# Four edits in a two-layer graph network: a type mask read from a table, a leaky ReLU through TensorE, node stores on ScalarE's queue, and sums begun by a copy

## The chip, the cores and the metric

The kernel runs on one core of a Trainium2 chip. The metric is the time of one execution on the device, in microseconds (us). The kernel before has a median of 4184.74 us over three runs (4179.8 to 4191.42). In this text PE is the matrix engine (TensorE), DVE the vector engine, ACT the scalar engine, POOL the GpSimd engine and SP the sync engine, which here does little but start transfers. DRAM is the memory outside the core; SBUF and PSUM are the two memories on it.

## The reference

There are 6250 nodes with 128 features and 106,250 edges, sorted by destination. The second layer takes the same edge list. Cut to what is computed (`relu`, `leaky` and `segment` functions written short):

```python
h = relu(layernorm(x))
for r in range(4):                              # edge types; 8 heads of 16 features
    xr = (h @ W_rel[r]).reshape(N, 8, 16)
    es, ed = (xr * a_src[r]).sum(-1), (xr * a_dst[r]).sum(-1)
    logit = leaky(es[src] + ed[dst], 0.2)
    logit = where(edge_type == r, logit, -1e30)
    p = exp(logit - segment_max(logit, dst)[dst]) * (edge_type == r)
    alpha = p / segment_sum(p, dst)[dst]
    out_r = segment_sum(alpha * xr[src], dst) + bias[r]
    h_r = gelu(out_r) @ W_cross
ent = stack([h @ W_self, h_0, h_1, h_2, h_3])   # 5 x N x 128
# a softmax over these five per node and head (types without an edge at a node left out)
x = x + sum_k(alpha_k * ent[k]) + bias_lang

h = relu(layernorm(x))
src2, dst2, ef2 = concat(src, dst), concat(dst, src), concat(ef, ef)
msg = leaky(concat(h[src2], h[dst2], ef2) @ We1, 0.01) @ We2
red = segment_sum(msg, dst2)
x = x + leaky(concat(h, red) @ Wn1, 0.01) @ Wn2
```

## The kernel before

**Tiling.** Nodes are cut into 50 blocks of 126 (two halves of 63, so 100 halves). The edges of a half are at most 1152, nine tiles of 128. Four halves make a superblock: 25 superblocks of nine steps. In each step one tile of each of the four halves is handled, so a step has four gathers and layer 1 has 900.

**Preparation** (0 to 167 us in the profile). The edge lists are loaded as 128x832 arrays on SP's queue, `x` on ACT's. DVE makes small edge tables in DRAM (`e2`, `turnd`, `dtyp`: what node and type an edge has, where a run of equal destinations ends). The first edge of each half is found (`st0`). Then 50 blocks of node rows go through layer norm and PE, and the projected rows of all four types are stored as a table `xt`, the node's own rows as `own`. Last, the indices of the gathers (`xi`) and the one-hot keys (`key`) are turned into place.

**Layer 1** (167 to 1578 us). `gather0` fetches the rows of `xt` for the edges, by an indirect DMA that POOL issues (L81), 17 tiles ahead of their use (18 buffers, `xg`). While superblock s has its messages made, superblock s + 1 has its softmax prepared:

- `loads`, two superblocks ahead, on SP's queue: for each of the four halves a slice of `turnd` (tile `t`), of `dst` and of `dtyp` spread over 64 partitions (`db`, `dt`), and of the edge types spread over four partitions (`et`).
- `masks`: DVE compares `et` with the partition's type number `tycf` (L508), which gives `ne`, 1 where an edge has another type; and `db` with the node numbers (L512), which gives the one-hot `oT`.
- `logits`, in three chunks of 384 edges: PE adds, in one PSUM bank `lg`, −1e30 times `ne` (L523), the destination's part (L525) and, after an ACT copy `es` for each tile, the source's part. There is one buffer of `lg`. The leaky ReLU is the larger of lg and 0.2 lg: ACT multiplies (L532), DVE takes the maximum (L533), both into `l`.
- `soft`: four scans of DVE along the edges with exponentials and a logarithm on ACT; `turn`: PE brings the weights to edges by partitions (`pt`).
- `messages`, each step of superblock s: DVE multiplies the gathered rows by the weights (L583), makes four one-hots (L590), and PE adds their products into `acc` (L591). `types` (L598) finds on ACT which types a node has.
- `nodes`, spread over the steps of the next superblock as a generator: gelu, the product with `W_cross`, the softmax over the five, the sum with ps in PSUM (copied to `y`), layer norm, and the second layer's products. It stores `y` to `x1r` (L684, two transfers), the two halves of the node table of layer 2 `abtab` (L703, four) and `h2t` (L704, one), all from SP's queue, behind a later point of the generator than that at which the data is made.

**Layer 2** (1578 to 4196 us). For each of 50 blocks and nine steps, POOL gathers two tiles of `abtab` rows (`ag`, ten buffers), PE makes the rest of the sum `z` (L1037) from the edge features `fe` and a one-hot of the destination (`db`, L999), DVE adds (L1039), ACT multiplies by 0.01 (L1040), DVE takes the maximum (L1041), and POOL stores the result row by row, sorted by the source node, to `m2d` (L1045). The destination's own sum is made by PE (`sums`, L1055), added to `racc` once a block (L1065). Behind each of five parts of the blocks, `windows` reads `m2d` back by source node and adds those sums to `racc` as well (L956). `racc` holds 50 blocks of 128x256 and is cleared by POOL before the layer (L924). After the last part, `node_update` makes the output, four blocks at a time.

**Order.** The order within the loops is written out by hand, as the generators and the step numbers above; a scheduler of the framework then orders the instructions of each engine by their dependences, and inserts the waits. Each engine and each queue runs in order.

Of the kernel before, what the change touches and what calls it, by code (L numbers as in the profile page):

```python
# [9 lines left out]
F32 = mybir.dt.float32  # L10
BF16 = mybir.dt.bfloat16
I32 = mybir.dt.int32
U8 = mybir.dt.uint8
AF = mybir.ActivationFunctionType
ALU = mybir.AluOpType
# [6 lines left out]
P = 128  # L22
# [4 lines left out]
R = 4  # L27
# [7 lines left out]
J = 832  # L35
# [50 lines left out]
def kernel(ctx: ExitStack, tc: tile.TileContext, x, src, dst, ef, et, w_rel, a_src, a_dst,  # L86
# [14 lines left out]
    def dram(name, shape, dt=F32):  # L101
        return nc.dram_tensor(name, shape, dt, kind="Internal").ap()
# [7 lines left out]
    turnd = dram("turnd", (2, JE + 8), BF16)  # L110
    dtyp = dram("dtyp", (1, JE))
    plcd = dram("plcd", (1, JE))
    m2d = dram("m2d", (E + TRASH, MW))
# [78 lines left out]
    with ExitStack() as prep:  # L192
# [84 lines left out]
        for k in range(2):  # L277
            nc.sync.dma_start(turnd[k, 1:JE + 1].rearrange("(p j) -> p j", j=J), dn[:, k, :])
            for o, w in ((0, 1), (JE + 1, 7)):
                nc.sync.dma_start(turnd[k:k + 1, o:o + w], dn[0:1, k, 0:w])  # L280
        dty = cpool.tile([P, J], F32, name="dty")
        stt(dty, dstf, float(R), ints["et"], op0=ALU.mult, op1=ALU.add)
# [150 lines left out]
    with ExitStack() as s1_:  # L433
# [6 lines left out]
        nc.gpsimd.iota(iota, [[1, R * 64]], base=0, channel_multiplier=0, allow_small_or_imprecise_dtypes=True)  # L440
        tyc = cp.tile([Q * R, 1], I32, name="tyc")
        nc.gpsimd.iota(tyc, [[0, 1]], base=0, channel_multiplier=1)
        ts_(tyc, tyc, R - 1, None, op0=ALU.bitwise_and)
        tycf = cp.tile([Q * R, 1], F32, name="tycf")
        nc.vector.tensor_copy(tycf, tyc)
        pen = cp.tile([Q * R, P], BF16, name="pen")
# [40 lines left out]
        def loads(s):  # L487
            ln = {}
            regs = first_of(st0, Q * s, Q, E - CAP)
            ln["t"] = wp.tile([2 * Q, CAP + 2], BF16, name="t")  # L490
            ln["et"] = wp.tile([Q * R, CAP], I32, name="et")
            ln["db"] = [wp.tile([P, CAP], I32, name="db") for _ in range(2)]
            ln["dt"] = [wp.tile([P, CAP], F32, name="dt") for _ in range(2)]
            for q in range(Q):
                r = regs[q]
                v, h0 = q // 2, (q % 2) * 64
                nc.sync.dma_start(ln["t"][2 * q:2 * q + 2, :], turnd[:, ds(r, CAP + 2)])
                nc.sync.dma_start(ln["db"][v][h0:h0 + 64, :], dst[ds(r, CAP)].partition_broadcast(64))
                nc.sync.dma_start(ln["et"][q * R:(q + 1) * R, :], et[ds(r, CAP)].partition_broadcast(R))
                nc.sync.dma_start(ln["dt"][v][h0:h0 + 64, :], dtyp[0, ds(r, CAP)].partition_broadcast(64))  # L500
            lanes[s] = ln

        def masks(s):

            ln = lanes[s]
            ln["a"] = wp.tile([P, CAP], F32, name="a", bufs=1)
            ln["ne"] = wp.tile([Q * R, CAP], BF16, name="ne", bufs=1)
            ts_(ln["ne"], ln["et"], tycf, None, op0=ALU.not_equal)  # L508
            ln["oT"] = []
# [7 lines left out]
        def logits(s, c):  # L517
# [9 lines left out]
            for i in range(3):  # L527
# [3 lines left out]
                                 start=False, stop=(i == 2), skip_group_check=True)  # L531
            nc.scalar.mul(ln["l"][:, e0:e1], lg, 0.2)  # L532
            tt(ln["l"][:, e0:e1], lg, ln["l"][:, e0:e1], op=ALU.max)  # L533

# [85 lines left out]
        def nodes(s, g, gt, last):  # L620

            e5 = wp.tile([P, R + 1, 2, C + H], F32, name="e5", bufs=1)
            rows = own[2 * s * P:(2 * s + 2) * P, :].rearrange("(v p) c -> p v c", v=2)
# [37 lines left out]
            y = wp.tile([P, 2, C], F32, name="y", bufs=1)  # L661
            nc.scalar.copy(y, ps)
            yield
            bn = wp.tile([P, 2, 6], F32, name="bn")
# [15 lines left out]
            for v in range(2):  # L680
                ts_(h2[:, v, :], ps[:, v, :], mv[:, v, 0:1], r[:, 0, v:v + 1], op0=ALU.subtract, op1=ALU.mult)
            x1q = x1r[2 * s * DB:(2 * s + 2) * DB, :].rearrange("(v q r) c -> q r v c", v=2, q=2)
            for q in range(2):
                nc.sync.dma_start(x1q[q], y[q * 64:q * 64 + GB])  # L684
            yield
# [3 lines left out]
            hT = wp.tile([P, 2 * P], F32, name="hT2")  # L689
            nc.scalar.activation(hT, tp, AF.Relu)  # L690
            yield

            ab = abtab[2 * s * DB:(2 * s + 2) * DB, :].rearrange("(v q r) f -> v q r f", v=2, q=2)
            for v in range(2):
                at = wp.tile([P, 2 * HID], F32, name="at")
                ps = bank(last)
                for a in range(2):
                    nc.tensor.matmul(ps[:, a * HID:(a + 1) * HID], hT[:, v * P:(v + 1) * P], wab[:, a, :],
                                     start=True, stop=True)
                nc.scalar.copy(at, ps)  # L700
                yield
                for q in range(2):
                    nc.sync.dma_start(ab[v, q], at[q * 64:q * 64 + GB])  # L703
            nc.sync.dma_start(h2t[:, 2 * s * P:(2 * s + 2) * P], hT)  # L704

# [207 lines left out]
    with ExitStack() as s4:  # L913
# [9 lines left out]
        col = col.rearrange("p q r -> p (q r)")  # L923
        nc.gpsimd.memset(racc, 0.0)  # L924

        def windows(j):
# [17 lines left out]
            for b in range(NU):  # L944
# [7 lines left out]
                for i in range(n):  # L952
                    oh = mp.tile([P, P], F32, name="ohw", bufs=4)
                    ts_(oh, col, at[:, i:i + 1], None, op0=ALU.is_equal)  # L954
                    nc.tensor.matmul(sums, oh, mt[:, i, 0:HID], start=(i == 0), stop=(i == n - 1))  # L955
                tt(racc[:, b, :], racc[:, b, :], sums, op=ALU.add)  # L956
                yield

        with ExitStack() as s5:
# [59 lines left out]
            for u in range(NU):  # L1019
# [43 lines left out]
                for _ in nxt_:  # L1063
                    pass
                tt(racc[:, u, :], racc[:, u, :], sums, op=ALU.add)  # L1065
            for _ in wins:
# [586 lines left out]
```

## Time and profile before

The profile is of one execution of 4198.35 us; its span (first to last instruction) is 4196.5 us, with 1.85 us around it. The median of the three timed runs is 4184.74 us.

| what | value |
|---|---|
| time, median of 3 (lowest, highest) | 4184.74 us (4179.8, 4191.42) |
| profiled execution, its span | 4198.35 us, 4196.5 us |
| mean granted TensorE clock | 0.848 |
| preparation, to the first gather | 0 to 167.2 us |
| layer 1, first to last gather | 167.2 to 1453 us |
| rest of layer 1 | 1453 to 1578.5 us |
| layer 2, first gather to POOL's last store | 1589.8 to 3993.8 us |
| last part and node update | 3993.8 to 4196.5 us |
| busy: PE, DVE, ACT, POOL | 3081.6, 2896.6, 1518.3, 2939.8 us |

How to read the profile's lines: the first line gives each engine's busy time, its share of the span and its number of instructions. A group line gives source line, engine, operation, result and operands by the program's names, the count, then busy time and the mean of one in ns, then the idle time of the engine just before them and what ended most of it. A line of the timeline gives start, length (us), engine, source line, operation, and in brackets the idle time before it with its releaser; "issue" is time in which the engine waited for nothing that the profile shows. L81 is the helper that issues every gather.

### The profile page before, as it was taken

The page shows a single profiled execution, that of the slowest core. Times are in us where ns is not written, and L with a number is a line of the kernel's source. Part 1 is how long each engine was busy: PE and PEld are TensorE (multiplying, and loading weights), DVE is VectorE, ACT ScalarE, POOL GpSimd, SP SyncE. Part 2 cuts the span into 40 slices and gives each one's busy share as a digit, 9 for nine tenths or more (in the row PEclk, how much of TensorE's full clock was granted, in tenths as well). Part 3 has the DMA queues.
Part 4 walks back from the last instruction along what each step waited for, and adds up shares of the span by engine and source line. Part 5 has one row for each costly group of instructions (what it writes and reads, how often), then busy time and mean ns, then how long its engine had stood idle before and what let it go on. Part 6 is the DMA issues. An engine that isn't in the chain of part 4 may idle for free. (4 is left out here: it accounts for less than half of the span.)

```text
span 4196.5 us, 43288 instructions
## 1 busy us (share of the span) xinstructions
PE 3081.6 (73%) x11108; PEld 1776.0 (42%) x11108; DVE 2896.6 (69%) x5392; ACT 1518.3 (36%) x2861; POOL 2939.8 (70%) x2889
## 2 busy tenths in 40 slices
PE   3457777777777765666677877778768777688888
PEld 2345555555555552222234433344324333244455
DVE  6777899999887764455566666566656666577755
ACT  2256655665555532222222322222222222222211
POOL 4777777777777607777777777777777777777700
PEclk9767888778778777888889999889988998899999
DMA  6645544444445317666678887787868878588754
GB/s 169 166 100 119 114 116 116 114 116 115 112 114 121 91 47 208 175 172 181 171 216 240 252 247 208 220 257 239 241 193 259 246 238 248 170 262 272 242 163 137
DMA packets 414125, 754.31 MB, mean 180 GB/s; under 512 B 182798, under 2 KB 248948, under 8 KB 413868
## 3 DMA queue, kind: packets, MB, share of 16 engines
q0 software_dynamic: 148800, 430.91, 35.4%
q1 hardware_dynamic: 247350, 307.89, 27.9%
q10 hardware_dynamic: 17718, 12.66, 1.2%
q8 instruction: 91, 1.49, 0.1%
q14 instruction: 166, 1.36, 0.1%
HBM read 587.35 MB, written 163.84 MB: 179 GB/s over the span
## 5 line engine op out<-in xcount | busy, mean ns | idle before, releaser
L81 POOL DMA_INDIRECT xg<-xt,xi x900 | 1005.1, 1117 | 280.8 <-issue 232.3
L1045 POOL DMA_INDIRECT m2d<-s,placei x900 | 915.8, 1018 | 288.7 <-issue 210.7
L81 POOL DMA_INDIRECT ag<-abtab,srci x900 | 911.4, 1013 | 288.2 <-issue 205.2
L1037 PE MATMUL z<-rhs,lt 128*128 128x512 f32 x1800 | 1041.1, 706 | 0.6 <-ACT lt L1008 0.6
L1041 DVE TENSOR_TENSOR s<-s,z 128x1024 f32<-128x1024 f32 x450 | 548.1, 1220 | 555.2 <-ACT z L1040 553.6
L1055 PE MATMUL sums<-s,oh 128*64 128x256 f32 x1800 | 335.7, 455 | 491.7 <-DVE s L1041 490.6
L1039 DVE TENSOR_TENSOR s<-z,ag 128x1024 f32<-128x1024 f32 x450 | 549.1, 1221 | 194.2 <-PE z L1037 169.4
L1040 ACT ACTIVATE z<-s 128x1024 f32<-128x1024 f32 x450 | 460.8, 1024 | 431.6 <-DVE s L1039 431.3
L591 PE MATMUL acc<-oh,msg 128*128 128x256 f32 x1800 | 527.4, 438 | 72.8 <-DVE oh L590 54.2
L1037 PEld LDWEIGHTS z<-rhs,lt 128*128 128x128 f32 x1800 | 353.8, 217 | 450.1 <-issue 445.1
L955 PE MATMUL sums<-mt,ohw 128*128 128x256 f32 x2024 | 525.6, 393 | 8.9 <-DVE ohw L954 8.9
L1042 ACT COPY s<-srcf 128x2 f32<-128x2 f32 x450 | 86.7, 193 | 1212.3 <-DMA m2d<-s,placei 1198.7
L955 PEld LDWEIGHTS sums<-mt,ohw 128*128 128x128 f32 x2024 | 391.5, 199 | 199.8 <-issue 130.2
L591 PEld LDWEIGHTS acc<-oh,msg 128*128 128x128 f32 x1800 | 372.4, 220 | 168.7 <-DVE oh L590 84.9
L1055 PEld LDWEIGHTS sums<-s,oh 128*64 128x64 f32 x1800 | 98.7, 149 | 732.8 <-DVE s L1041 549.1
L590 DVE TENSOR_SCALAR oh<-iota,key 128x256 f32<-128x256 f32 x900 | 303.7, 361 | 60.2 <-PE acc L591 56.3
L598 ACT ACTIVATE junk<-dt,nthr 128x1152 bf16<-128x1152 f32 x250 | 312.9, 1252 | 5.7 <-issue 3.5
L954 DVE TENSOR_SCALAR ohw<-col,at 128x128 f32<-128x128 f32 x1012 | 249.1, 298 | 19.3 <-PE sums L955 11.0
L583 DVE TENSOR_TENSOR msg<-xg,pt 128x512 f32<-128x512 f32 x225 | 148.8, 675 | 75.8 <-PE pt L576 69.5
L1004 PE MATMUL tp<-ident,fe 128*128 128x128 f32 x450 | 85.6, 295 | 137.4 <-ACT lt L1008 114.7
L1008 ACT COPY lt<-tp 64x384 f32<-64x384 f32 x300 | 141.8, 473 | 109.3 <-PE tp L1004 62.8
L576 PE MATMUL pt<-sel,l 128*128 128x32 f32 x450 | 94.2, 383 | 88.3 <-ACT l L568 88.2
(278 smaller groups left out, 3369.3 us busy)
## 6 DMA issues: line engine op xcount, KB each, us to landing
mt<-m2d SPq DMA_DIRECT2D x156, 514.0 KB
db<-in_dst_dram SPq DMA_DIRECT2D x200, 288.0 KB
mt<-m2d SPq DMA_DIRECT2D x53, 642.5 KB
dt<-dtyp SPq DMA_DIRECT2D x100, 288.0 KB
fe<-in_edge_attr_dram SPq DMA_DIRECT2D x100, 288.0 KB
mt<-m2d SPq DMA_DIRECT2D x41, 385.5 KB
xg<-xt,xi POOLq DMA_INDIRECT x900
ag<-abtab,srci POOLq DMA_INDIRECT x900
```

What stands on the lines that cost most here:

```text
L81: nc.gpsimd.indirect_dma_start(out=o, out_offset=None, in_=table, in_offset=bass.IndirectOffsetOnAxis(ap=idx.bitcast(I32), axis=0))
L590: ts_(oh.rearrange("p t n -> p (t n)"), iota, key[:, k:k + 1], None, op0=ALU.is_equal)
L591: nc.tensor.matmul(acc[q // 2][:, :, q % 2, :], msg[:, q, :], oh, start=(i == 0 and q % 2 == 0), stop=(i == TB - 1), skip_group_check=True)
L598: nc.scalar.activation(junk, lanes[s]["dt"][v], AF.Sign, bias=nthr[:, u, t:t + 1], accum_out=g[:, v, t:t + 1])
L954: ts_(oh, col, at[:, i:i + 1], None, op0=ALU.is_equal)
L955: nc.tensor.matmul(sums, oh, mt[:, i, 0:HID], start=(i == 0), stop=(i == n - 1))
L1037: nc.tensor.matmul(z[:, q, :], lt[q][:, i * P:(i + 1) * P], rhs[(2 * u + q) % 4], start=True, stop=True)
L1039: tt(s[:, :, 0:2 * HID], z, ags.pop(n), op=ALU.add)
L1040: nc.scalar.mul(z, s[:, :, 0:2 * HID], 0.01)
L1041: tt(s[:, :, 0:2 * HID], s[:, :, 0:2 * HID], z, op=ALU.max)
L1045: st = nc.gpsimd.indirect_dma_start(out=m2d, out_offset=bass.IndirectOffsetOnAxis(ap=placei[:, k:k + 1], axis=0), in_=s[:, q, HID:HID + MW ...
L1055: nc.tensor.matmul(sums[q * 64:(q + 1) * 64, :], oh[:, q * TB + i, :], s[:, q, 0:HID], start=(i == 0), stop=(i == TB - 1))
```

## The change

- A DRAM table `lacks` of four rows (one a type) is made in the preparation: four DVE comparisons of the edge types with 0, 1, 2 and 3, and four stores on SP's queue. In layer 1 the slices of `lacks` are loaded as `ne`, in place of `et`; the comparison L508, the type numbers `tyc` and `tycf` and the loads of `et` are gone.
- The leaky ReLU is computed as 0.2 (lg + 4 max(lg, 0)): ACT makes 4 max(lg, 0) into `l`, PE adds it to `lg` by a product with the identity, and ACT multiplies by 0.2 into `l`. DVE's maximum is gone.
- The stores of `nodes` go from SP's queue to ACT's, each right behind the ACT instruction that makes its data. `e5` has two buffers in place of one.
- `racc` isn't cleared. The first sums of a block are copied there by ACT, later ones are added by DVE, as before (`add_sums`).

```diff
+    lacks = dram("lacks", (R, JE), BF16)
...
+        for r in range(R):
+            ne = wpool.tile([P, J], BF16, name="ne")
+            ts_(ne, ints["et"], float(r), None, op0=ALU.not_equal)
+            nc.sync.dma_start(lacks[r].rearrange("(p j) -> p j", j=J), ne)
...
-        tyc = cp.tile([Q * R, 1], I32, name="tyc")
-        nc.gpsimd.iota(tyc, [[0, 1]], base=0, channel_multiplier=1)
-        ts_(tyc, tyc, R - 1, None, op0=ALU.bitwise_and)
-        tycf = cp.tile([Q * R, 1], F32, name="tycf")
-        nc.vector.tensor_copy(tycf, tyc)
...
-            ln["et"] = wp.tile([Q * R, CAP], I32, name="et")
+            ln["ne"] = wp.tile([Q * R, CAP], BF16, name="ne")
...
-                nc.sync.dma_start(ln["et"][q * R:(q + 1) * R, :], et[ds(r, CAP)].partition_broadcast(R))
+                nc.sync.dma_start(ln["ne"][q * R:(q + 1) * R, :], lacks[:, ds(r, CAP)])
...
-            ln["ne"] = wp.tile([Q * R, CAP], BF16, name="ne", bufs=1)
-            ts_(ln["ne"], ln["et"], tycf, None, op0=ALU.not_equal)
...
-            nc.scalar.mul(ln["l"][:, e0:e1], lg, 0.2)
-            tt(ln["l"][:, e0:e1], lg, ln["l"][:, e0:e1], op=ALU.max)
+
+            l = ln["l"][:, e0:e1]
+            nc.scalar.activation(l, lg, AF.Relu, scale=4.0)
+            nc.tensor.matmul(lg, ident, l, start=False, stop=True, skip_group_check=True)
+            nc.scalar.mul(l, lg, 0.2)
...
-            e5 = wp.tile([P, R + 1, 2, C + H], F32, name="e5", bufs=1)
+            e5 = wp.tile([P, R + 1, 2, C + H], F32, name="e5")
...
             nc.scalar.copy(y, ps)
+            x1q = x1r[2 * s * DB:(2 * s + 2) * DB, :].rearrange("(v q r) c -> q r v c", v=2, q=2)
+            for q in range(2):
+                nc.scalar.dma_start(x1q[q], y[q * 64:q * 64 + GB])
...
-            x1q = x1r[2 * s * DB:(2 * s + 2) * DB, :].rearrange("(v q r) c -> q r v c", v=2, q=2)
-            for q in range(2):
-                nc.sync.dma_start(x1q[q], y[q * 64:q * 64 + GB])
...
             nc.scalar.activation(hT, tp, AF.Relu)
+            nc.scalar.dma_start(h2t[:, 2 * s * P:(2 * s + 2) * P], hT)
...
                 nc.scalar.copy(at, ps)
+                for q in range(2):
+                    nc.scalar.dma_start(ab[v, q], at[q * 64:q * 64 + GB])
                 yield
-                for q in range(2):
-                    nc.sync.dma_start(ab[v, q], at[q * 64:q * 64 + GB])
-            nc.sync.dma_start(h2t[:, 2 * s * P:(2 * s + 2) * P], hT)
...
-        nc.gpsimd.memset(racc, 0.0)
+        begun = set()
+
+        def add_sums(b, sums):
+
+            if b in begun:
+                tt(racc[:, b, :], racc[:, b, :], sums, op=ALU.add)
+            else:
+                nc.scalar.copy(racc[:, b, :], sums)
+                begun.add(b)
...
-                tt(racc[:, b, :], racc[:, b, :], sums, op=ALU.add)
+                add_sums(b, sums)
...
-                tt(racc[:, u, :], racc[:, u, :], sums, op=ALU.add)
+                add_sums(u, sums)
```

## The prediction

> **What bounds the kernel now.** I read the busy times first, then the groups by cost, the windows of layer 1, and last the timelines of POOL and DVE where the diff touches the work.
>
> ```profile
> PE 3081.6 (73%) x11108; PEld 1776.0 (42%) x11108; DVE 2896.6 (69%) x5392; ACT 1518.3 (36%) x2861; POOL 2939.8 (70%) x2889
> ...
> L81 POOL DMA_INDIRECT xg<-xt,xi x900 | 1005.1, 1117 | 280.8 <-issue 232.3
> L1045 POOL DMA_INDIRECT m2d<-s,placei x900 | 915.8, 1018 | 288.7 <-issue 210.7
> L81 POOL DMA_INDIRECT ag<-abtab,srci x900 | 911.4, 1013 | 288.2 <-issue 205.2
> ```
>
> POOL is busy 70 % of the span, but each indirect transfer costs it about 0.3 us more, released by "issue", that is, by nothing but itself. Layer 1 has 900 gathers: 1005.1 + 280.8 = 1285.9 us, from 167.2 to 1452.9. Layer 2 has 1800: 915.8 + 288.7 + 911.4 + 288.2 = 2404 us, from 1589.8 to 3993.8. In these two stretches a saving counts only if POOL gets it. Outside them (0 to 167, 1452.9 to 1589.8, from 3993.8) other engines set the end.
>
> ```profile
> 850.00:900.00 50.00, 39.49 (x157) 27.97 (x157) 44.45 (x95) 31.33 (x56) 40.25 (x33) 0.73 0.45 108
> 1450.00:1500.00 50.00, 40.97 (x164) 30.40 (x163) 29.86 (x93) 20.08 (x36) 2.30 (x3) 0.74 0.36 81
> 1500.00:1550.00 50.00, 32.51 (x135) 25.84 (x134) 34.21 (x79) 18.06 (x30) 0.00 (x0) 0.73 0.07 19
> ```
>
> Columns: window, length, then PE, PE's loads, DVE, ACT, POOL, the granted clock, the DMA share, GB/s. In mid layer 1 (about one superblock of 36 gathers per 50 us) DVE is 89 % busy and PE 79 %, POOL 40.25 + 33 x 0.3 = 50 us: full. Once the gathers stop, no engine is full: a chain of waits sets the pace. ACT has 19 us of 50 free, DVE 5.5: the change moves work from DVE to ACT and PE.
>
> **1. The type mask `ne` from a table.** Removed: 25 DVE instructions (L508) and the loads of `et`. Added: four DVE passes over 128x832 and four stores of 213 KB in the preparation. The diff's `ne` loads move 2 bytes a type where those of `et` moved 4.
>
> ```profile
> L508 DVE TENSOR_SCALAR ne<-et,tycf x25: 782/801/951, 206.2 to 1491.0; 16x1152 bf16<-16x1152 int32 x25
> ```
>
> That is 25 x 0.80 = 20 us of DVE, but not of the path. What POOL gets is seen beside it:
>
> ```profile
> 899.42 2.54 DVE L551 TENSOR_TENSOR_SCAN f<-km,l 128x1152 f32<-128x1152 f32 x1
> ...
> 899.63 0.95 POOL L81 DMA_INDIRECT xg<-xt,xi  x1 [0.30 <-issue]
> ...
> 900.88 0.95 POOL L81 DMA_INDIRECT xg<-xt,xi  x1 [0.30 <-DMA xg<-xt,xi]
> ...
> 929.86 0.87 DVE L508 TENSOR_SCALAR ne<-et,tycf 16x1152 bf16<-16x1152 int32 x1
> ...
> 929.95 1.17 POOL L81 DMA_INDIRECT xg<-xt,xi  x1 [0.31 <-DVE oh L590]
> ```
>
> Beside L508 a gather takes 1.17; beside a scan that reads PSUM it takes 0.95, the shortest there is. The mean gather, 1117 ns, is 167 ns over the median 950: 900 x 0.167 = 150 us that POOL loses, some beside L508. At 0.22 each: 25 x 0.22 = 5.5 us; bounds 0 (the next DVE instruction stands there in its place) and 25 x 0.80 = 20 (stopped throughout). I take 7, near the row.
>
> The Trainium skill ("SBUF — State Buffer", section "Who interferes with whom") says that a tensor_scalar in a two-port mode holds the pair shared with GpSimd for the whole instruction, and that instructions with at most one SBUF input outside those modes do not contend. By the rule L508 would cost a gather up to its whole 0.80, an estimate of 20 us, and the sum below would be 13 us lower; the row shows 0.22.
>
> Preparation: a 128x832 pass takes 584 ns in the nearest row (L762), so 4 x 0.58 = 2.3 us of DVE, which is 33 of the first 50 us busy; two of the four stand ahead of `holds`, all ahead of the block starts. 0.85 MB at the 208 to 226 GB/s of the first 30 us is 4 us of transfer beside the loads of x. I take +3 (0, if the later row pipeline to 155 covers it, to +5).
>
> **2. Leaky ReLU.** Removed: 75 DVE maxima (L533). Added per chunk: one product with the identity and one ACT pass (Relu, then the multiplication by 0.2 that was there).
>
> ```profile
> L533 DVE TENSOR_TENSOR l<-lg,l x75: 518/546/558, 212.1 to 1506.6; 128x384 f32<-128x384 f32 x75
> ```
>
> 75 x 0.546 = 41 us leave DVE, 1.6 us a superblock. L533 reads one PSUM and one SBUF operand, as the scan does beside which gathers take 0.95: for POOL 0 (to −5, the lengthening that falls beside it). ACT gets 75 x 0.49 (L532's own row), PE 75 x 0.45 to 0.9 (four passes of L525's 128x384 take 0.87 on end; two to four are needed). A superblock then has ACT 31 + 1.5, PE 39.5 + 2.5, both under 50 us. PE's new product stands in order behind ACT's Relu, and every message product behind it; the order of the changed kernel leaves 2 to 12 message products of 0.44 us before it, 0.9 to 5.3 us, against Relu 0.49 plus whatever ACT is in (a `types` pass, L598, takes 1.25). Mostly covered.
>
> DVE's room brings something where it is late: one gather starts late for want of a free buffer.
>
> ```profile
> 511.96 1.05 POOL L81 DMA_INDIRECT xg<-xt,xi  x1 [5.05 <-issue]
> ```
>
> I take −4 for this and two gaps of 1.2 us (0 to −7). With `ne` gone, −7, the gathers' stage gives −11 (−2 to −22).
>
> **3. The tail of layer 1**, 1452.9 to 1578.5, no gathers.
>
> ```profile
> 1437.96 2.56 DVE L551 TENSOR_TENSOR_SCAN f<-km,l 128x1152 f32<-128x1152 f32 x1
> ...
> 1461.79 0.69 DVE L583 TENSOR_TENSOR msg<-xg,pt 128x512 f32<-128x512 f32 x1 [3.67 <-PE pt L576]
> ```
>
> Superblock 22's first message starts at 1404.2, that of 23 at 1461.8: 57.6 us later, against 50.5 between 21 and 22. Superblock 22's last message starts at 1423.0, the first scan of 23's softmax at 1438.0: DVE has few one-hots (L590) left, and the scans run alone. In the changed order five one-hots stand behind that scan (none before), and 15 to 16 message products behind the last logits product (10 to 16 before, none in this superblock). I take −7, the difference to 50.5; bounds 0 and −15 (1438 − 1423). The last superblock's three chunks are uncovered (no message products stand behind its last logits product): each loses L533's 0.55 and gains a Relu, a product and, once, a `types` pass between them: 3 x (0.49 + 0.5 − 0.55) + 1.4 = +2.7, less what starts earlier: +1.5 (−2 to +6).
>
> **4. The stores on ACT's queue.** Seven issues of 0.30 to 0.36 us a superblock leave SP (L684, L703, L704) and go right behind the ACT instruction that makes their data; `e5` gets a second buffer, which lets its load go earlier: 0. On ACT 7 x 0.33 = 2.3 us a superblock: 31 + 1.5 + 2.3 = 35 of 50. What ACT queues behind them: the `es` copies, exponentials and gelus of the superblock. On SP the loads for two superblocks ahead are no longer behind stores. In mid stage 0. At the end the last `abtab` store leaves SP at 1575.96 and POOL resumes when it has landed, at 1578.53; issued 0.3 us earlier or later it moves that by as much: 0 (±1).
>
> The Trainium skill ("DMA: Bandwidth & Descriptors", section "Issuing engines are not separate DMA queues") says that starting DMAs on another engine saves only issue time, since all interleave on the same sixteen engines: by it this part brings nothing but ACT's 2.3 us, which speaks against it. No row here shows otherwise, and the sum keeps 0.
>
> **5. `racc` not cleared.**
>
> ```profile
> 1451.96 0.95 POOL L81 DMA_INDIRECT xg<-xt,xi  x1 [0.31 <-issue]
> ...
> 1578.53 0.19 POOL L918 IOTA iota<- 128x64 f32 x1 [125.62 <-DMA abtab<-at]
> ...
> 1578.88 10.76 POOL L924 MEMSET racc<- 128x12800 f32 x1
> ...
> 1589.83 1.31 POOL L81 DMA_INDIRECT ag<-abtab,srci  x1 [0.15 <-issue]
> ...
> 1604.69 1.01 POOL L1045 DMA_INDIRECT m2d<-s,placei  x1 [1.72 <-DVE s L1041]
> ```
>
> 10.76 us go from POOL alone. But POOL can run only ten gathers ahead (five pairs of `ag` buffers), 13 us, and then stands until the first store's rows exist:
>
> ```profile
> 1597.56 1.23 DVE L1039 TENSOR_TENSOR s<-z,ag 128x1024 f32<-128x1024 f32 x1 [4.43 <-PE z L1037]
> ```
>
> L1039 waits for PE's first product, that for the one-hot rows from `fe` and `db`, whose loads left SP at 1578.97 and later and landed near 1591.6. None of that moves with the memset: 1597.56 + 1.23 + L1040 1.02 + L1041 1.22 + 0.5 = 1601.5 is the earliest for the first store, against 1604.69. So −3.2, and a little because DVE's L999 at 1585.62, 4.67 us beside the memset and 0.81 otherwise, shortens: −4 (0 if the loads land late, −10.8 if they land early).
>
> Copies for adds: the first touch of each of 50 blocks takes ACT 0.37 (128x256, the `y` copy) for DVE's 0.41. Beside POOL's 2404 us, ACT 22 % busy: 0 (±4, from the 28 us of extra gaps there). Without POOL's cover it would be 50 x 0.04 = 2 us.
>
> **Sum** against the profiled execution's 4198.35 (span 4196.5, and 1.85 around it): +3 − 11 − 7 + 1.5 + 0 − 4 + 0 = −17.5, giving 4181. That execution is 13.6 over the median 4184.74; a median of the changed kernel is then 4184.74 − 17.5 = 4167; I say 4166. With the ends joined as independent, 4150 to 4180.
>
> **Rivals.**
> - *ACT's in-order queue delays the consumer (slower).* A store on ACT waits for a semaphore, and in the changed order what precedes its turn is often one of SP's loads two superblocks ahead; SP's own L991 at 1582.61 stood 3.1 us for such a landing. Behind it on ACT stand `es` copies, for which PE and DVE wait. For: seven a superblock, DVE and PE 80 to 89 % busy. Against: ACT has 15 us free of 50. It decides when ACT's work and waits pass about 52 us a superblock, i.e. 17 us of waits, five stores standing 3.1 us each. At 3 us over in each of 25 superblocks: 4167 + 75 = 4242.
> - *PE's order (slower).* The identity product waits behind Relu and holds the message products. PE has 39.5 + 2.5 of 50; it decides at 8 us of standing a superblock, 2.7 us per chunk. Two us over: 4167 + 50 = 4217.
> - *Nothing arrives (same).* DVE's next instruction lengthens the gathers instead, the loads land late at the boundary, the preparation pays 5: about 4185.
> - *All arrives.* Gathers −22, tail −15, boundary −10.8, preparation 0: −48, and +1.5 in the last superblock: 4138.
>
> **How the numbers follow.** Forecast 0.53, all arrives 0.10, nothing 0.13, ACT's queue 0.14, PE's order 0.10. A measurement of this kernel tells about 0.3 %, 12.6 us, from no change: faster is under 4172. From the forecast 0.10 lies above that, so faster 0.43 + 0.10 + 0.02 = 0.55; same 0.10 + 0.11 = 0.21; slower 0.24, the two slow rivals. The range 4142 to 4222 leaves out most of ACT's queue and half of all arrives, about 2 in 10. The forecast's own range is 4150 to 4180.
>
> **What would show it.** Right: gathers of layer 1 below 1117 ns mean, last gather near 1442; POOL idle 118 to 122 us after it; first store some 4 us closer to the last `abtab` landing; layer 2's 2404 us unchanged. Wrong: ACT with waits for DMA in front of its stores and `es`, gaps of over 1 us on POOL in layer 1, PE idle before the identity product by more than 8 us a superblock, or a layer 2 that moves by more than 4 us.

## The result and the profile after

The changed kernel takes 4181.2 us (median of 12 runs, 4167.78 to 4193.52), against 4190.73 for the kernel before in 12 runs beside it: a ratio of 0.9976, with a 95 % interval from 0.9964 to 0.9987. That is 9.5 us faster (5 to 15), about half of the 17.5 that were forecast. The sign was right, and the time lies in the stated range of 4142 to 4222, but 1 us above the forecast's own, 4150 to 4180; and with 12.6 us from no change as the mark that the prediction set, it counts as "same" (0.21), not as "faster" (0.55). Ratios, here and below, leave out the few executions that lie over 1.5 % above the fastest of the same kernel; the medians keep them. The two profiled executions stand 25.9 us apart (4198.35 and 4172.47), because that of before lies 7.6 us above its median and that of after 8.7 below: some 16 us of the difference between the two traces is the luck of single executions.

Its page, the lines that answer to those shown of the kernel before:

```profile
PE 3111.7 (75%) x11258; PEld 1790.3 (43%) x11258; DVE 2830.8 (68%) x5244; ACT 1574.8 (38%) x2994; POOL 2899.4 (70%) x2887
...
L81 POOL DMA_INDIRECT xg<-xt,xi x900 | 980.5, 1089 | 289.0 <-issue 237.8
L81 POOL DMA_INDIRECT ag<-abtab,srci x900 | 907.4, 1008 | 303.4 <-issue 203.0
L1054 POOL DMA_INDIRECT m2d<-s,placei x900 | 913.9, 1015 | 288.6 <-issue 213.7
```

DVE lost 66 us of work and ACT and PE gained 56 and 30, in the direction that the diff says. The gathers of layer 1 became shorter (1089 ns in place of 1117: 24.6 us in all), but POOL's idle time before them grew by 8.2 us (289.0 against 280.8). The windows of layer 1 and of the stretch after its last gather (columns as before):

```profile
850.00:900.00 50.00, 35.11 (x136) 24.44 (x134) 40.91 (x74) 28.22 (x47) 38.62 (x33) 0.76 0.42 94
1435.00:1485.00 50.00, 41.35 (x165) 29.40 (x164) 26.10 (x86) 25.30 (x51) 0.00 (x0) 0.81 0.27 68
1485.00:1535.00 50.00, 34.32 (x142) 27.87 (x141) 33.09 (x84) 15.88 (x26) 0.00 (x0) 0.72 0.08 22
```

The stages of the profiled executions, and what had been forecast for each:

| stage | before | after | difference | forecast |
|---|---|---|---|---|
| to the first gather | 167.2 | 164.2 | −3.1 | +3 |
| gathers of layer 1 | 1285.7 | 1269.2 | −16.5 | −11 |
| last gather to the first iota of layer 2 | 125.6 | 123.1 | −2.5 | −5.5 |
| iota to the first store of layer 2 | 26.2 | 33.5 | +7.3 | −4 |
| first to last store of layer 2 | 2389.1 | 2380.3 | −8.8 | 0 |
| last store to the end | 202.7 | 200.5 | −2.3 | 0 |

The −8.8 between the stores can't be told from the spread of single executions: over the traces of all kernels that take about 4185 us this stage is 2377 to 2390 us long.

Layer 2's start went the wrong way. PE's first uses of the loaded `fe` and its first product there, in the trace before:

```profile
1591.66 0.87 PE L1004 MATMUL tp<-ident,fe 128*128 128x128 f32 x3 [17.03 <-DMA db<-in_dst_dram]
1593.10 2.07 PE L1037 MATMUL z<-rhs,lt 128*128 128x512 f32 x2 [0.56 <-ACT lt L1008]
```

POOL's and PE's lines in the trace after:

```profile
1556.43 0.19 POOL L919 IOTA iota<- 128x64 f32 x1 [123.08 <-DMA abtab<-at]
...
1557.12 1.75 POOL L81 DMA_INDIRECT ag<-abtab,srci  x1 [0.30 <-issue]
...
1577.01 0.87 PE L1013 MATMUL tp<-ident,fe 128*128 128x128 f32 x3 [24.18 <-DMA ag<-abtab,srci]
1578.45 2.07 PE L1046 MATMUL z<-rhs,lt 128*128 128x512 f32 x2 [0.56 <-ACT lt L1017]
...
1584.40 1.41 POOL L81 DMA_INDIRECT ag<-abtab,srci  x1 [14.07 <-DVE s L1048]
...
1589.91 1.16 POOL L1054 DMA_INDIRECT m2d<-s,placei  x1 [0.30 <-issue]
```

The 10.76 us of clearing are gone and the gathers start 0.7 us behind the iota, but POOL then stands 14.07 us: PE's first product comes 22.0 us behind the iota, against 14.6 before (1593.10 − 1578.53).

### The profile page after: what moved, and what is told of

Its sections match the earlier page's. It is cut to its first block, busy times and chain, and to the rows that moved or that the text cites. A ratio compares the mean times of both kernels' runs of the same rounds, so it can differ in the third digit from the quotient of the medians.

```text
span 4170.7 us, 43560 instructions
## 1 busy us (share of the span) xinstructions
PE 3111.7 (75%) x11258; PEld 1790.3 (43%) x11258; DVE 2830.8 (68%) x5244; ACT 1574.8 (38%) x2994; POOL 2899.4 (70%) x2887
## 5 line engine op out<-in xcount | busy, mean ns | idle before, releaser
L81 POOL DMA_INDIRECT xg<-xt,xi x900 | 980.5, 1089 | 289.0 <-issue 237.8
L81 POOL DMA_INDIRECT ag<-abtab,srci x900 | 907.4, 1008 | 303.4 <-issue 203.0
L592 PE MATMUL acc<-oh,msg 128*128 128x256 f32 x1800 | 501.9, 421 | 71.1 <-DVE oh L591 51.4
L592 PEld LDWEIGHTS acc<-oh,msg 128*128 128x128 f32 x1800 | 363.3, 212 | 164.3 <-DVE oh L591 74.0
L963 DVE TENSOR_SCALAR ohw<-col,at 128x128 f32<-128x128 f32 x1012 | 250.5, 299 | 19.5 <-PE sums L964 11.3
L1013 PE MATMUL tp<-ident,fe 128*128 128x128 f32 x450 | 86.6, 299 | 138.1 <-ACT lt L1017 107.2
L1013 PEld LDWEIGHTS tp<-ident,fe 128*128 128x128 f32 x450 | 58.9, 151 | 212.3 <-ACT lt L1017 140.8
```

The costliest lines, as they stand in the source:

```text
L81: nc.gpsimd.indirect_dma_start(out=o, out_offset=None, in_=table, in_offset=bass.IndirectOffsetOnAxis(ap=idx.bitcast(I32), axis=0))
L592: nc.tensor.matmul(acc[q // 2][:, :, q % 2, :], msg[:, q, :], oh, start=(i == 0 and q % 2 == 0), stop=(i == TB - 1), skip_group_check=True)
```

## The experiments

All ratios are to the kernel before, measured among the same runs. One thing must be known to read them: in three of the five groups of runs (e1 to e4, e13 to e16, e17 and e18) every kernel took longer. The kernel before took 4896 to 4979 us there in place of 4185, at a granted clock of 0.78 to 0.81 in place of 0.84 to 0.87, so times are compared within a group only. (The expectations put this down to a slower chip; but the chip of e9 to e12 was the same as that of e17 and e18.) I call them the long groups. Their layer 1 is limited in another way, as the page of one of them (e16) shows:

```profile
PE 3241.8 (65%) x11108; PEld 1834.1 (37%) x11108; DVE 2887.7 (58%) x5342; ACT 1535.8 (31%) x2911; POOL 2868.6 (58%) x2888
...
L81 POOL DMA_INDIRECT xg<-xt,xi x900 | 953.4, 1059 | 748.7 <-issue 570.0
```

POOL is idle 748.7 us before its gathers in layer 1 (280.8 in the profile of before). Of these, 458 us are long waits that end 0.74 us behind the multiplication (L583) that frees the buffer for the next gather: there the consumer, that is, the engines that work on the gathered rows, sets the pace, not POOL. So a saving of POOL's time gains nothing there by itself. Why the consumer is late is open: during the gathers of e16 ACT stands over 8 us 30 times, 492 us in all, against 6 times and 91 us in the trace of before, mostly for something that the profile does not name.

| run | parts of the change | ratio | 95 % interval | us |
|---|---|---|---|---|
| e5 | all four | 0.9973 | 0.9960 to 0.9986 | 4175.2 |
| e6 | all but stores (and `e5`'s buffer) | 1.0006 | 0.9994 to 1.0018 | 4187.8 |
| e7 | all, and the clearing too | 0.9955 | 0.9939 to 0.9970 | 4168.4 |
| e8 | all but leaky ReLU | 0.9941 | 0.9926 to 0.9957 | 4163.0 |
| e9 | table, stores, two `e5` | 0.9935 | 0.9919 to 0.9950 | 4152.7 |
| e10 | as e9, weights loaded late | 0.9936 | 0.9923 to 0.9949 | 4158.3 |
| e11 | stores, one `e5` | 1.0042 | 1.0029 to 1.0055 | 4202.3 |
| e12 | table | 0.9960 | 0.9945 to 0.9974 | 4168.5 |
| long: e1 | table | 1.0037 | 1.0005 to 1.0070 | 5001.9 |
| long: e2 | leaky ReLU | 1.0042 | 1.0012 to 1.0072 | 4996.2 |
| long: e3 | stores, one `e5` | 1.0264 | 1.0217 to 1.0310 | 5113.0 |
| long: e4 | sums by copies | 0.9980 | 0.9954 to 1.0005 | 4971.8 |
| long: e13 | table, two `e5`, stores on SP | 0.9946 | 0.9919 to 0.9973 | 4944.8 |
| long: e14 | table, stores, one `e5` | 1.0025 | 0.9990 to 1.0060 | 4975.3 |
| long: e15 | leaky ReLU | 1.0063 | 1.0033 to 1.0094 | 5001.1 |
| long: e16 | sums by copies | 1.0004 | 0.9967 to 1.0040 | 4973.7 |
| long: e17 | as e13 | 0.9881 | 0.9836 to 0.9926 | 4842.3 |
| long: e18 | as e14 | 0.9983 | 0.9947 to 1.0019 | 4896.4 |

The kernel before is at 4185.23 beside e5 to e8 and at 4184.22 beside e9 to e12.

**e5, the changed kernel again.**

> The changed kernel again, beside the kernel before on this chip. If the parts add up as on the slower chip of the four runs before (table +0.4 %, leaky ReLU +0.4 %, stores on ACT +2.6 %, sums -0.2 %), it is 3 % slower there and about 0.2 % faster on a chip like that of the profile. Theory of the prediction: the same 0.2 to 0.5 % faster on any chip.

It was 10 us faster again. The parts did not carry over from the long group; nothing is to be added across groups.

**e1 and e12, the table alone.** The edit is the change's hunks on `lacks`, `ne` and `tycf`:

```diff
-            ts_(ln["ne"], ln["et"], tycf, None, op0=ALU.not_equal)
...
+                nc.sync.dma_start(ln["ne"][q * R:(q + 1) * R, :], lacks[:, ds(r, CAP)])
```

> The kernel before with the type mask from the table alone (four comparisons and stores in the preparation, loads of the table in layer 1, no L508). Theory of the prediction: the preparation +3 us, the stage of the gathers of layer 1 -7 (down to -20 if a gather stands for the whole of L508's 0.80 us), rest unchanged: -4 us in all. Rival (DVE's next instruction takes L508's place beside the gathers): the gathers' stage within 3 us of before, the total within 3 us. The profiled pair of kernels had the first gather 3 us earlier, not later, in the changed kernel; if that comes from this part, the preparation is -3 here too.

> The kernel before with the type mask from the table alone, as in the run on the slower chip, where it cost 0.4 %. Theory of the prediction: 4 us faster. From the sum of the other parts on this kind of chip (-10 in all, less -12.6 for the stores, +12.2 for the leaky ReLU, +6.7 for the clearing): 16 us faster. Rival (DVE's next instruction stands in its place): within 3 us.

Where POOL is the bound (e12), the table alone is 16.7 us faster (11 to 23). Where POOL is not (e1), it gains nothing and costs 0.4 %. POOL's line of e12:

```profile
L81 POOL DMA_INDIRECT xg<-xt,xi x900 | 982.7, 1092 | 279.3 <-issue 222.1
```

A gather is 25 ns shorter than before, 900 x 0.025 = 22 us, and the idle time before it is unchanged within 2 us: in the profiled execution the gathers' stage is 1261.7 us long, 24 less. So the rival falls, and my −7 was too small. How much of the 22 us comes from the missing L508 itself is not shown: in e11 (below), where L508 is in place and only the engines' order and the stores' queue differ from before, a gather takes 1101 ns, 16 less than before, so the order moves this mean as well. The first gather is at 165.7 us (167.2 before; 164.2 to 168.5 over the traces of all kernels): the four comparisons and stores of the preparation cost nothing that shows.

**e2, e15 and e8, the leaky ReLU alone, and everything but it.**

```diff
-            nc.scalar.mul(ln["l"][:, e0:e1], lg, 0.2)
-            tt(ln["l"][:, e0:e1], lg, ln["l"][:, e0:e1], op=ALU.max)
+            l = ln["l"][:, e0:e1]
+            nc.scalar.activation(l, lg, AF.Relu, scale=4.0)
+            nc.tensor.matmul(lg, ident, l, start=False, stop=True, skip_group_check=True)
+            nc.scalar.mul(l, lg, 0.2)
```

e8 is the changed kernel with the removed two lines in place of the added four.

> The kernel before with the leaky ReLU by Relu, identity product and ACT alone. Theory of the prediction: gathers' stage -4 us (DVE's room), tail of layer 1 -5.5 us (superblock 23 -7, last superblock +1.5), total -9.5 us. Rival (the chain through ACT, PE and ACT is longer than the one through ACT and DVE, and superblocks start later): the gathers' stage 0 to +10 us, tail 0 to +5, total slower by 0 to 15 us.

> The leaky ReLU's new form alone on the kernel before, as on the slower chip (+0.4 % there). Theory of the prediction: 9.5 us faster. From its removal from the changed kernel (12 us faster without it): 12 us slower, with the consumer of layer 1 further behind at the last gather (the last es copy 15 to 20 us behind a superblock's last gather, 4 to 12 before) and a tail of layer 1 of over 130 us.

> The changed kernel with the leaky ReLU by ACT and DVE's maximum as before. Theory of the prediction: 9.5 us slower than the changed kernel (gathers' stage 4, tail 5.5). Rival (the longer chain through PE costs what DVE's room gains): within 3 us of the changed kernel; or faster, if the chain costs more.

Without this part the changed kernel is 12.2 us faster (0.9941 against 0.9973; the intervals do not overlap), and alone it is 0.4 and 0.6 % slower in the long groups. The part is a loss. POOL's gathers, first of the changed kernel (e5), then of e8:

```profile
L81 POOL DMA_INDIRECT xg<-xt,xi x900 | 984.0, 1093 | 288.7 <-issue 231.1
```

```profile
L81 POOL DMA_INDIRECT xg<-xt,xi x900 | 1003.2, 1115 | 274.2 <-issue 218.1
```

Without DVE's maximum the gathers take 19.2 us less. But 14.5 of these come back as waits for free buffers (288.7 against 274.2; each wait over 0.5 us ends 0.74 us behind the multiplication that frees the buffer), so that the stage is 4.7 us shorter, 1272.5 against 1277.2. The loss lies behind it. The last gather, the last `es` copy and the iota, of e5 and then of e8:

```profile
1436.68 0.95 POOL L81 DMA_INDIRECT xg<-xt,xi  x1 [0.30 <-issue]
...
1478.52 0.49 ACT L527 COPY es<-xg 128x128 f32<-128x128 f32 x2
...
1555.11 0.19 POOL L919 IOTA iota<- 128x64 f32 x1 [117.48 <-DMA abtab<-at]
```

```profile
1441.99 0.95 POOL L81 DMA_INDIRECT xg<-xt,xi  x1 [0.30 <-issue]
...
1476.39 0.28 ACT L527 COPY es<-xg 128x128 f32<-128x128 f32 x1
...
1549.79 0.19 POOL L916 IOTA iota<- 128x64 f32 x1 [106.85 <-DMA abtab<-at]
```

I take the end of the last `es` copy behind the end of the last gather as the consumer's lag. With the new form it is 41.4 us (1479.01 − 1437.63), without it 33.7 (1476.67 − 1442.94); from there to the iota it is 76.1 and 73.1. The tail is 10.6 us longer: 7.7 of lag and 3.0 of chain. Over superblocks 3 to 22 the last `es` copy is 16.4 us behind a superblock's last gather with it, 8.8 without.

This pair of traces differs by 6 us only, half of the 12.2 of the medians. But up to layer 2 the engines' orders of e8, e9 and e10 are the same, and so are those of the changed kernel, e5 and e7, so that three traces stand against three:

| us | old form: e8, e9, e10 | new form: changed kernel, e5, e7 |
|---|---|---|
| gathers, busy | 1003.2, 994.2, 998.3 | 980.5, 984.0, 978.8 |
| idle before gathers | 274.2, 274.2, 274.3 | 289.0, 288.7, 286.6 |
| gathers' stage | 1277.2, 1268.2, 1272.4 | 1269.2, 1272.5, 1265.2 |
| consumer's lag at the last gather | 33.7, 31.4, 32.9 | 45.9, 41.4, 46.0 |
| last gather to the iota | 106.9, 103.5, 107.2 | 123.1, 117.5, 123.1 |

In the mean the stage is 3.6 us shorter and the tail 15.4 longer, 11.8 together, as the medians say. The lag also differs over superblocks 3 to 22: 8.8 to 10.7 us with the old form, 16.4 to 16.5 with the new.

What makes the consumer late is seen in the last chunk. In e5, from Relu to the scan that needs the logits:

```profile
1480.15 0.48 ACT L532 ACTIVATE l<-lg 128x384 f32<-128x384 f32 x1
1480.52 1.26 ACT L599 ACTIVATE junk<-dt,nthr 128x1152 bf16<-128x1152 f32 x1
...
1480.69 1.65 PE L533 MATMUL lg<-l,ident 128*128 128x384 f32 x2 [1.11 <-ACT l L532]
...
1482.37 0.49 ACT L534 ACTIVATE l<-lg 128x384 f32<-128x384 f32 x1 [0.50 <-PE lg L533]
...
1482.90 2.56 DVE L552 TENSOR_TENSOR_SCAN f<-km,l 128x1152 f32<-128x1152 f32 x1 [0.62 <-ACT l L534]
```

And in e8, from the multiplication to the same scan:

```profile
1477.95 0.49 ACT L530 ACTIVATE l<-lg 128x384 f32<-128x384 f32 x1
...
1478.47 0.56 DVE L531 TENSOR_TENSOR l<-lg,l 128x384 f32<-128x384 f32 x1 [4.77 <-ACT l L530]
1479.06 2.56 DVE L549 TENSOR_TENSOR_SCAN f<-km,l 128x1152 f32<-128x1152 f32 x1
```

1.11 us became 2.75: one pass of DVE gave way to a product in two passes on PE (1.65 together here; a pass takes 0.49 in the median of the trace) and one more pass of ACT. Over all 75 chunks, from the start of the first ACT pass to the finished logits, it is 3.7 us in the mean in the three traces with the new form and 2.5 in the three without. That this lengthening makes the lag is the nearest reading; how 1.2 us a chunk add up to some 7 us of lag was not followed step by step.

**e3, e11, e6, e13, e14, e17 and e18: the stores' queue and `e5`'s buffer.** The part has two edits:

```diff
-            e5 = wp.tile([P, R + 1, 2, C + H], F32, name="e5", bufs=1)
+            e5 = wp.tile([P, R + 1, 2, C + H], F32, name="e5")
...
-                nc.sync.dma_start(x1q[q], y[q * 64:q * 64 + GB])
+                nc.scalar.dma_start(x1q[q], y[q * 64:q * 64 + GB])
```

with the stores of `h2t` and `abtab` in the same way. Without the table's smaller tiles there is no room for the second buffer, so that e3 and e11 have one.

> The kernel before with the stores of nodes on ACT's queue alone (e5 keeps one buffer, since without the smaller mask tiles a second one has no room). Theory of the prediction: 0 (within 2 us in each stage). Rival (ACT's stores wait for landings of SP's loads and hold the es copies): the gathers' stage longer by 5 to 30 us. Second rival (SP's loads were late behind the stores): gathers' stage shorter by 3 to 10 us.

> The kernel before with the stores of nodes on ACT's queue alone (one buffer of e5), as in the run on the slower chip, where it cost 2.6 %. If SP's loads were late behind the stores, 8 to 13 us faster than before, in the gathers' stage and the tail of layer 1; if the gain needs the table's shorter loads or e5's second buffer, within 3 us of before; theory of the prediction: 0.

> The changed kernel with the stores of nodes back on SP's queue, at their old places. Theory of the prediction: the stores' queue is worth 0, so the same time as the changed kernel within 3 us. Rival (ACT's stores wait for landings and hold up the es copies): 10 to 130 us faster than the changed kernel, in the stage of the gathers of layer 1.

> The table part with a second buffer of e5, and the stores still on SP. If the gain of the stores' part (14 us beside the table) is the buffer's, the time of the table with both, about 4153; if it is the queue's, the time of the table alone, about 4168. Theory of the prediction: the buffer is worth 0, as is the queue.

> The table part with the stores on ACT's queue and one buffer of e5. If the queue brings the gain, 4153 to 4158; if the queue alone costs what it cost without the table (18 us), 4186; theory of the prediction: 4168, as the table alone.

> The table part with a second buffer of e5 and the stores on SP, which was 0.5 % faster than before on the slower chip, where the table alone was 0.4 % slower. On a chip like that of the profile: if the gain of the stores' part is the buffer's, 4150 to 4156 (ratio 0.9925 to 0.994, as the table with both); if it is the queue's, 4168 (0.996, as the table alone).

> The table part with the stores on ACT's queue and one buffer of e5, 0.25 % slower than before on the slower chip. If the gain is the buffer's, at or above the table alone (4168, ratio 0.996); if it is the queue's, 4150 to 4156.

Together the two edits are worth 12.6 us in the changed kernel (e6 against e5) and 15.8 beside the table (e9 against e12, same group). Alone, the queue loses: 18 us in e11, 130 in a long group (e3). In the long groups the two were separated: the second buffer with the stores on SP is faster than before by 0.5 and 1.2 % (e13, e17), the queue with one buffer is not faster than before (e14, e18). So there the buffer brings the gain, and the queue beside one buffer none. The queue beside two buffers was not run in the long groups, and in the groups of the ordinary time the split was not measured; that the queue alone loses 18 us there speaks for the same. The `L81` line of e11 shows the loss as waits for buffers (303.4 us idle, 280.8 before):

```profile
L81 POOL DMA_INDIRECT xg<-xt,xi x900 | 990.8, 1101 | 303.4 <-issue 249.8
```

ACT standing for landings, as the rival had it, is not what the trace of e11 names: from 170 to 1440 us ACT's waits that a landing other than a gather's ended sum to 9 us.

Where the two edits' gain shows can be said: the consumer's lag at the last gather is 46.3 us in e12 and 31.4 in e9, and the time from there to the iota 78.2 and 72.1, so that the tail is 21 us shorter (124.5 and 103.5), while the gathers' stage is 6.5 us longer. In the changed kernel the lag is 50.1 in e6 and 41.4 in e5.

Why the buffer helps stays open. It changes more than one wait: the scheduler places everything anew, and between the traces of e12 and e13 (same but for the buffer) 404 of PE's 11108 instructions and 416 of DVE's 5369 stand at another place in the order. One sign of it is ACT's changes of its function table (1.28 us each): during the gathers 130 in e11, 123 in e12 and in the changed kernel, 115 in e9, and in the kernel before 115 as well, so that they alone do not order the times.

**e4, e16 and e7: the clearing.** e4 and e16 have the copies and no clearing, on the kernel before. e7 is the changed kernel and does the clearing too, for nothing:

```diff
+        nc.gpsimd.memset(racc, 0.0)
         begun = set()
```

> The kernel before with racc begun by copies and not cleared, alone. Theory of the prediction: 4 us shorter from the layer's first iota on POOL to the end of the 20th indirect transfer (38.9 us before), nothing afterwards, total -4 us. Rival (the clearing was cover for the first block's loads, which now share the DMA engines with the gathers): PE's first product z at 20 to 23 us after the iota (14.6 before, 22.0 in the changed kernel), the 20th transfer ends 39 to 42 us after it, total within 3 us of before.

> The copies for the clearing alone on the kernel before, as on the slower chip (-0.2 % there). Theory of the prediction: 4 us faster. From putting the clearing back (7 us faster with it): 0 to 7 us slower, with PE's first product of layer 2 at 20 to 23 us after the iota (14.6 before). Layer 1 is that of the kernel before, so its stages also show how far those of one execution vary.

> The changed kernel with POOL's clearing of racc put back (10.76 us of POOL) and the copies kept, so that the clearing is work for nothing. Theory of the prediction: 4 us slower. Rival (the clearing is cover for the first block's loads): PE's first product z back at 14 to 16 us after the layer's first iota (22.0 in the changed kernel), the 20th indirect transfer ends 38 to 41 us after it as in the changed kernel, total within 3 us of the changed kernel.

10.76 us of POOL put back did not make the kernel slower: 4168.4 against 4175.2, where the intervals overlap, so no difference can be claimed either way. e7's start of layer 2:

```profile
1554.17 0.19 POOL L919 IOTA iota<- 128x64 f32 x1 [123.15 <-DMA abtab<-at]
...
1554.52 10.76 POOL L925 MEMSET racc<- 128x12800 f32 x1
...
1565.47 1.31 POOL L81 DMA_INDIRECT ag<-abtab,srci  x1 [0.15 <-issue]
...
1568.99 2.07 PE L1047 MATMUL z<-rhs,lt 128*128 128x512 f32 x2 [0.56 <-ACT lt L1018]
```

PE's first product is back at 14.8 us behind the iota (22.0 and 22.1 without the clearing in the changed kernel and in e5, 20.6 and 21.0 in e4 and e16), and the 20th indirect transfer ends at 40.4 (41.0 without it in e5; 38.9 before; 39.5 and 39.2 in e4 and e16). So the clearing's time is nearly free: it covers the wait for the first block's loads, and without it the gathers run beside these loads. The one trace without the clearing that gains is e6, with the stores on SP: its first product comes 16.2 us behind the iota and its 20th transfer ends at 36.1, 2.8 us sooner than before. In the trace after, the packets of `fe` for the second half have landed 19.3 us behind the iota (1575.69), in that of before 11.3 (1589.80), though SP issues them 8.8 and 8.2 us behind it; in e7 they land at 11.6, in e6 at 13.4.

**e9 and e10, what the runs point to.** e9 is the kernel before with the table, the stores on ACT and two buffers of `e5`; leaky ReLU and clearing stay as they were. e10 also loads three weights of the node update late:

```diff
-    nc.scalar.dma_start(w2, we2.rearrange("(a k) f -> k a f", k=P))
...
+        nc.scalar.dma_start(w2, we2.rearrange("(a k) f -> k a f", k=P))
         wp = s4.enter_context(tc.tile_pool(name="l2w", bufs=2))
```

> The kernel before with two of the four parts: the type mask from the table, and the stores on ACT's queue with two buffers of e5. If the four runs on this kind of chip add up (changed kernel -10 us, without the leaky ReLU's new form a further -12, with the clearing back a further -7), it is 29 us (0.7 %) faster than before: about 4156. Theory of the prediction (table -4, stores 0): 4 us faster than before. From the end of the gathers of layer 1 to the layer's first iota 104 to 110 us (125.6 before, 106.8 in the changed kernel with DVE's maximum); PE's first product of layer 2 14 to 16 us after the iota.

> The same two parts, and the three weight loads of the node update (w2, wn1t, wn2t, 0.5 MB on ACT's queue) moved from the start of layer 2 to just before the node update. If the start of layer 2 is bound by the loads that share the DMA engines, 0.5 MB at some 230 GB/s is 2.2 us: PE's first product 2 us earlier after the iota than in the kernel with the two parts alone, total 2 us less; if the first gathers or the one-hots bound it, no difference.

e9 is 0.65 % faster than before (0.50 to 0.81 %), 4152.7 us: the best of the kernels measured outside the long groups, and near where the sum of the parts put it (4156). From its last gather to the iota it is 103.5 us:

```profile
1432.41 1.00 POOL L81 DMA_INDIRECT xg<-xt,xi  x1 [0.30 <-issue]
...
1536.91 0.19 POOL L916 IOTA iota<- 128x64 f32 x1 [103.50 <-DMA abtab<-at]
```

e10 is the same within its interval; its first product is 13.6 us behind the iota, against 14.0. The half megabyte of weights is not what the start waits for.

## Why the prediction was right in sign and wrong in size

By removal and alone, the parts are worth about −17 (table), +12 (leaky ReLU), −13 (stores and buffer) and 0 to +7 (no clearing), each within some 6 to 8 us: −11 to −18 in sum, against −10 for all four. The forecast had −4, −9.5, 0 and −4 for the same parts. That the total came within a factor of two is luck: two terms were too pessimistic and two too optimistic, and none of the four was right in size.

- *Part 1, "At 0.22 each ... I take 7".* The term was mis-sized: −16.7 in e12. I read one light row, 1.17 beside L508. The 34 gathers that overlap the 25 L508 in the trace before take 1317 ns in the mean, 12.5 us over 34 x 950 in all, some of which belongs to their other neighbours. From the Trainium skill's rule in "SBUF — State Buffer", section "Who interferes with whom", the prediction had an estimate of 20 us, and the measured 11 to 23 lies nearer to that than to my row. But 12.5 is the most that L508's own neighbours give; the table also moved the order of the engines, so the runs neither confirm the rule nor show the port alone.
- *Part 1, "+3" in the preparation.* Wrong; the lower bound held, 0.
- *Part 2, "Mostly covered" and, in part 3, "I take −7".* This is the step that failed most: −9.5 forecast, +12 found. What failed is the tail: −5.5 forecast, +15.4 found over three traces against three. I took it for the two last superblocks' own overlap, while its length depends on the lag that the consumer carries at the last gather, and the new form adds about 12 us to that (31 to 34 became 41 to 46). The last superblock's chain came near (+3.7 against +1.5). The gain at the gathers, −3.6 against −4, is right by luck: I had it from shorter waits for buffers, but these grew by 14 us, and the gathers themselves, for which I had put 0 (to −5), took 17.5 us less. My own sign of being wrong, gaps of over 1 us on POOL, came: six in the trace after, three before, none in e8 to e10. The rival "PE's order" had the sign but not the cause that it named: PE stands 5.0 us in all before the 75 identity products of the trace after, 0.2 a superblock, where it asked for 8. The lag need not stop POOL to show in the tail.
- *Part 4, "0 (±1)" and, of the second buffer, "lets its load go earlier: 0".* Both were wrong, with opposite signs (the buffer's as far as the long groups show it). The queue alone loses (+18), with the sign of the rival on ACT's in-order queue, but at less than its price and without the waits that it named; both edits together gain 13 to 16. The Trainium skill's rule on issuing engines ("DMA: Bandwidth & Descriptors", section "Issuing engines are not separate DMA queues") promised the queue nothing but the issue time. That the queue gains nothing agrees with e14 and e18; the loss of 18 us in e11 is not in the rule.
- *Part 5, "None of that moves with the memset".* Wrong: PE's first product moved from 14.6 to 22.0 us behind the iota. My bound "0 if the loads land late" was the case in all traces without the clearing but e6 (−2.8); the clearing had been the loads' cover. The rival "nothing arrives" had it.
- *Copies for adds, 0.* Nothing shows: from the first store to the last, layer 2 takes 2377 to 2390 us over the traces of all kernels but those of the long groups.
- *Expected signs.* Gathers under 1117 ns came (1089), a last gather near 1442 too (1433), and POOL was idle 123 us after it (118 to 122 forecast); the first store closer to the iota did not.

## What to carry to other kernels

When a transfer engine runs ahead of its consumer, price a change of the consumer by its lag, too: a delay that does not stop the leader shows when the leader ends. Work that fills a wait can be free, so find out what the wait is for before the filler is counted as a gain. And where a scheduler writes the order, a change of a buffer count is a change of the program: measure the parts of a bundle one by one, since here one of four lost most of what another gained, and one brought nothing.

## What the runs showed that was not expected

- One chip gave 4184 us for the kernel before in one group of runs and 4896 in another. In the long groups the preparation (to the first gather, 164.5 to 168.5 us) and the last part (200 to 203 us) are as long as ever; nearly all of the time more is in the two layers: the gathers' stage takes 1646 to 1876 us there (1262 to 1294 otherwise), first to last store of layer 2 2693 to 2744 (2377 to 2390). The cause was not looked for.
- Single executions of kernels with the start of layer 2 of the kernel before differ by 13 us from its iota to its last store (2404.8 to 2417.8 in e9, e11, e12 and the trace of before): two profiles alone could have given each part of this change a wrong size.
